# FP4 feed-forward stage in one fixed instruction order: output transposes inside a later tile's last quarter, input transposes between output products

## The chip, the cores and the metric

The kernel runs on one core of a Trainium2 chip. The metric is the device time in microseconds of one execution, the median of several runs. The kernel before has a median of 2238.77 us in three runs (2237.82 to 2240.83).

A core has five engines that run their own queues in order: TensorE (PE), VectorE (DVE), ScalarE (ACT), GpSimd (POOL) and SyncE (SP, which issues the DMAs here). They wait for each other through semaphores.

## What is computed

Two layers of gated cross attention and feed-forward over x (8 x 224 rows of 512). Only the last feed-forward is touched by the change:

```python
def fp4_quant_dequant(x):            # blocks of 16 along the last dim
    scale = max(|xb|) / 6, at least 1e-12
    q = nearest of {0, .5, 1, 1.5, 2, 3, 4, 6} to |xb / scale|, sign kept
    return q * scale
gate = fp4(x) @ fp4(w_gate).T        # 512 -> 1408
y    = fp4(x) @ fp4(w_up).T          # 512 -> 1408
h    = silu(gate) * y
out  = x + tanh(g) * (fp4(h) @ fp4(w_down).T)     # 1408 -> 512
```

In the kernel fp4 of x is taken after a layernorm. All products are in float32; each matrix product of the program is two records (two MATMUL and two LDWEIGHTS) in the profile, a transpose is one.

## The kernel before

**The stage.** The 1792 rows are 14 tiles of 128 rows (`NF`). A tile f goes through four functions:

- `ffn1_in` (L1035): a DMA loads x, three DVE passes and a POOL pass make the layernorm's statistics, a DVE pass normalizes, `fp4_steps` quantizes 512 columns, four PE transposes (L1055) go into a PSUM tile, and `evac` (L85) copies them into `xqT`, alternating between ACT and DVE.
- `ffn1_hidden` (L1059): the 1408 hidden columns are four quarters of 352. For each, four gate products (`wg`) go into one half of a PSUM tile and four up products (`wu`) into the other half, all at L1066. ACT makes a tanh of the gate half (L1077), DVE multiplies it with the gate half (L1078), and after the up products DVE multiplies with the up half (L1080) into h. In the last stage `banks` (L1172) hands out one PSUM tile `ps_big` for both halves, from a pool of two.
- `fp4_steps` (L939) on h, in two pieces of 704 columns: eight DVE passes (L959, L960, L961, L964, L967, L971, L972, L973) and one POOL pass (L974).
- `ffn1_out` (L1085): eleven PE transposes of h (L1092) in groups of 4, 4 and 3 through the PSUM tiles `th` and `t` (one buffer each), ACT copies into `hqT` (L1093), eleven output products of 512 columns with `wd` (L1097), a DVE add (L1109) and the store.

These functions are generators: each `yield` is a place where other work may be put in between.

**Order of the work.** `ffn1` (L1164) loops over tiles 2 to 13. One turn emits the hidden part of tile f, the input of tile f + 1, the quantization of h of tile f, and the output of tile f - 2, one after the other; the outputs of tiles 12 and 13 follow the loop. Tiles 0 and 1 have their input and hidden parts in `ffn1_first` (L1112) and `ffn1_head` (L1130), inside the last attention batch. There the two halves have separate PSUM tiles (L1154).

The emitted order is not the executed one everywhere. The framework schedules instructions and adds the semaphore waits. `pin` (L208) chains the PE, DVE and ACT instructions emitted so far in their order. It is called at L1305, before the last stage: what comes ahead of that keeps the order of the code, the last stage is ordered by the scheduler. In the order that results, the scheduler puts some gate products of the next quarter ahead of the up products of a quarter, and splits transposes and output products among them.

**Pace.** In the attention of the second layer `pace` (L251) takes pieces from the queue `beside` until the DVE work that is owed reaches a number of us, 3.5 at L652.

Of the kernel before, what the change touches and what calls it, by code (L numbers as in the profile page):

```python
# [26 lines left out]
F32 = mybir.dt.float32  # L27
# [7 lines left out]
B, S, D = 8, 224, 512  # L35
# [27 lines left out]
class Net:  # L63
# [492 lines left out]
    def attention8(self, n, soon, values, queue, beside):  # L556
# [50 lines left out]
        for slot in range(KC * NT):  # L607
            g, i = divmod(slot, NT)
            sc = [self.ps("half", [TP, 2, 512]) for _ in rows]
            for c in range(2):  # L610
                for h, r in enumerate(rows):
                    nc.tensor.matmul(  # L612
                        sc[h][:, c, :MH],
                        lhsT=qT[r, g, i * TP : (i + 1) * TP],
                        rhs=kT[g][r, c * MH : (c + 1) * MH],
                        start=True,
                        stop=True,
                    )
            nms = []
            for h in range(2):  # L620
                src = sc[h][:, :, :MH]
                mx = self.small.tile([TP, 1], F32, name="mx")
                nc.vector.tensor_tensor_reduce(  # L623
                    out=src,
                    in0=src,
                    in1=masks[i],
                    scale=1.0,
                    scalar=-MASKED,
                    op0=ALU.add,
                    op1=ALU.max,  # L630
                    accum_out=mx,
                )

                nms.append(self.small.tile([TP, 1], F32, name="nm"))
                nc.vector.tensor_scalar(nms[h], mx, -1.0e38, -1.0, ALU.max, ALU.mult)  # L635
            self.behind = 0
            if not soon:
                self.pace(1.5, beside)
            if slot == 4:
                next(first)  # L640
            p = self.weights_room(TP, M)
            for h, us in enumerate((1.6, 1.0)):
                self.fill(us, queue)
                nc.scalar.activation(  # L644
                    p[:, h, :].rearrange("p (c k) -> p c k", c=2),
                    sc[h][:, :, :MH],
                    AF.Exp,
                    bias=nms[h],
                    accum_out=total[:, i, h, g : g + 1],
                )  # L650
            if not soon:
                self.pace(3.5, beside)  # L652
            self.fill(1.6, queue)
            if slot == 3:
                first = divided(0)
                next(first)
            if slot == 4:
                next(first)
            if slot == 1:
                self.finish(values)  # L660
            if slot:
                product(*before)
            if slot == 4:
                next(first)
            pT = self.weights_room(CP, NKT * TP)
            for h in range(2):
                pt = self.ps("half", [CP, 2, 512])
                half = NKT // 2
                for j in range(NKT):
                    nc.tensor.transpose(  # L670
                        pt[:, j // half, j % half * TP : (j % half + 1) * TP],
                        p[:, h, j * CP : (j + 1) * CP],
                        self.ident[:TP, :TP],
                    )
                nc.scalar.copy(  # L675
                    pT[:, h, :].rearrange("p (c k) -> p c k", c=2), pt[:, :, : half * TP]
                )
            before = g, i, pT
            self.finish(soon)
            self.fill(1.2 if n < 2 * B - 1 else 3.0, queue)  # L680
# [354 lines left out]
    def ffn1_in(self, work, f, x, xn, xqT, bufs):  # L1035


        nc = self.nc
        nc.sync.dma_start(out=x, in_=self.last[f * TF : (f + 1) * TF, :])
        st = self.small.tile([TF, 6], F32, name="st1")  # L1040
        nc.vector.bn_stats(st, x)
        mv = self.small.tile([TF, 2], F32, name="mv1")
        nc.vector.bn_aggr(mv, st)
        ve = self.small.tile([TF, 1], F32, name="ve1")
        nc.vector.tensor_scalar(ve, mv[:, 1:2], EPS, None, ALU.add)
        rstd = self.small.tile([TF, 1], F32, name="rstd1")
        nc.gpsimd.tensor_tensor(rstd, ve, self.neghalf[:, 0:1], ALU.pow)
        yield 0, 1.2
        nc.vector.tensor_scalar(xn, x, mv[:, 0:1], rstd, ALU.subtract, ALU.mult)
        yield 0, 0.6  # L1050
        yield from self.fp4_steps(work, xn, xn, D, bufs)
        yield 0, 0, True
        pt = self.ps("t", [128, KC, TF])
        for k in range(KC):
            nc.tensor.transpose(pt[:, k, :], xn[:, k * 128 : (k + 1) * 128], self.ident)  # L1055
        self.evac(xqT, pt)
        yield 0.45, 0

    def ffn1_hidden(self, xqT, h, gate, banks):  # L1059
# [23 lines left out]
            yield 0.6, 0.6  # L1083

    def ffn1_out(self, pool, f, x, h, wd):  # L1085
        nc = self.nc
        hqT = pool.tile([128, NC1, TF], F32, name="hqT", bufs=2)

        def transposes(k0, k1, bank):
            pt = self.ps(bank, [128, k1 - k0, TF])  # L1090
            for k in range(k0, k1):
                nc.tensor.transpose(pt[:, k - k0, :], h[:, k * 128 : (k + 1) * 128], self.ident)  # L1092
            nc.scalar.copy(hqT[:, k0:k1, :], pt)  # L1093

        def products(k0, k1):
            for k in range(k0, k1):
                nc.tensor.matmul(  # L1097
                    po, lhsT=hqT[:, k, :], rhs=wd[:, k, :], start=k == 0, stop=k == NC1 - 1
                )


        transposes(0, 4, "th")
        transposes(4, 8, "t")
        po = self.ps("m", [TF, D])
        products(0, 4)
        transposes(8, NC1, "th")
        products(4, NC1)
        y = pool.tile([TF, D], F32, name="yout", bufs=2)
        nc.vector.scalar_tensor_tensor(y, po, self.gate[:, 3:4], x, ALU.mult, ALU.add)  # L1109
        nc.sync.dma_start(out=self.out[f * TF : (f + 1) * TF, :], in_=y)  # L1110
# [19 lines left out]
    def ffn1_head(self, work, beside):  # L1130
# [1 line left out]
        h = self.head  # L1132
        flat = self.wpool.tile([128, KC * D], F32, name="wv")
        h["h"].append(flat[:, :HID1])
        room = self.att.tile([128, KC, MH], F32, name="cx", bufs=2)
        room = room.rearrange("p k m -> p (k m)")
        at, there = 0, {}
        for name, width in (("a", D), ("e", D), ("most", D // BLK), ("scale", D // BLK), ("inv", D // BLK)):
# [3 lines left out]
        def quantized(h):  # L1142
            for c0 in range(0, HID1, D):
                part = h[:, c0 : min(c0 + D, HID1)]
                yield from self.fp4_steps(work, part, part, part.shape[1])

        for f in range(2):
            ahead = self.ffn1_in(there, f + 1, h["x"][f + 1], h["xn"], h["xqT"], 1)
            for i, cost in enumerate(
                self.ffn1_hidden(  # L1150
                    h["xqT"],
                    h["h"][f],
                    lambda: flat[:, HID1 : HID1 + CW],
                    lambda: [self.ps("m", [TF, CW]) for _ in range(2)],  # L1154
                )
            ):
                yield cost
                if i % 5 == 2 and i < 25:
                    yield next(ahead)
            yield from ahead  # L1160
            if f == 0:
                beside.append(quantized(h["h"][f]))

    def ffn1(self, pool, wd):  # L1164

        def quantized(h):
            for c0 in range(0, HID1, QW):
                self.fp4(pool, h[:, c0 : c0 + QW], h[:, c0 : c0 + QW], QW, 2)  # L1170

        def banks():  # L1172
            ps = self.ps("big", [TF, 2, 512])
            return ps[:, 0, :], ps[:, 1, :]

        x, h, xqT = self.head["x"], self.head["h"], self.head["xqT"]
        waiting = [(0, x[0], h[0]), (1, x[1], h[1])]
        x = x[2]
        quantized(h[1])
        for f in range(2, NF):  # L1180
            h = pool.tile([TF, HID1], F32, name="h", bufs=3)
            for _ in self.ffn1_hidden(
                xqT, h, lambda: pool.tile([TF, CW], F32, name="gth", bufs=2), banks
            ):
                pass
            waiting.append((f, x, h))
            if f + 1 < NF:
                x = pool.tile([TF, D], F32, name="xf", bufs=5)
                xn = pool.tile([TF, D], F32, name="xn1", bufs=2)
                xqT = pool.tile([128, KC, TF], F32, name="xqT1", bufs=2)  # L1190
                for _ in self.ffn1_in(pool, f + 1, x, xn, xqT, 2):
                    pass
            quantized(h)
            self.ffn1_out(pool, *waiting.pop(0), wd)
        for tile_ in waiting:
            self.ffn1_out(pool, *tile_, wd)

    def run(self):  # L1200
# [101 lines left out]
                self.weight("wo", sources[1]["wo"])  # L1302
        self.finish(beside)
        self.finish([rest, self.project_out(2 * B - 1)])
        self.pin()  # L1305
        prep.close()
        banks.close()
        right.close()
# [1 line left out]
        with ExitStack() as last:  # L1310
# [2 lines left out]
            wd = wdpool.tile([128, NC1, D], F32, name="wd")  # L1313
            self.nc.sync.dma_start(out=wd, in_=self.wd)
            self.ffn1(self.pool(last, "ffn1", side="right"), wd)


# [67 lines left out]
```

## Time and profile before

| what | value |
|---|---|
| median of three runs | 2238.77 us |
| the profiled execution's own time | 2234.42 us |
| its span, first to last instruction | 2232.6 us |
| mean granted PE clock | 0.998 |
| PE busy, share of the span | 2151.8 us, 96% |
| DVE busy | 1385.0 us, 62% |
| ACT busy | 699.2 us, 31% |
| POOL busy | 130.7 us, 6% |
| chain that ended last: PE | 84% |
| chain that ended last: DVE | 12% |
| last stage, loop over tiles 2 to 13 | 1828.35 to 2206.44 us |

How to read it: the span is cut by the profiler into instructions with a start and a duration for each engine. "Idle before" an instruction is followed by the instruction that released it. Matmuls overlap: a record of PE has its own length, about 0.17 us longer than the distance to the next one in a dense row, so rates are read from starts. PE's weight loads have a row of their own (PEld) and run beside products.

### The profile page before, as it was taken

Reading aid. Unit: us, or ns where it says so; the run is one execution under the profiler, and the core shown is the slowest. Engines: PE = TensorE matmul, PEld = TensorE weight load, DVE = VectorE, ACT = ScalarE, POOL = GpSimd, SP = SyncE. Lnnn points to the kernel's source line nnn. Section 1 sums busy time; section 2 is a strip of 40 time slices with the busy share of each in tenths; the row PEclk is TensorE's granted clock in tenths of the full one; section 3 lists DMA queues with packets and bytes.
Section 4 is the critical chain, followed back from the end, with each engine's and each line's share of the span. In section 5 each row is a group of like instructions: output and inputs, shape, how many; then the busy total and the mean of one; then the engine's idle time right before and its main releaser. Section 6 shows DMA issues by size and latency. Waiting matters only on the chain.

```text
span 2232.6 us, 33189 instructions
## 1 busy us (share of the span) xinstructions
PE 2151.8 (96%) x14062; PEld 1226.2 (55%) x14062; DVE 1385.0 (62%) x2618; ACT 699.2 (31%) x1173; POOL 130.7 (6%) x145
## 2 busy tenths in 40 slices
PE   7989899999999999999899999999999999999999
PEld 4444546364555546465656565665656555555554
DVE  3786767676766767773656565564523468666652
ACT  1222415151423325152543343343434321110111
POOL 0000000000000000000001010110000012111110
PEclk9999999999999999999999999999999999999999
DMA  6210010101000011101011212122110020000000
GB/s 218 67 38 29 1 45 2 31 15 30 16 18 29 7 39 39 63 2 63 3 38 57 63 28 64 41 67 66 37 36 15 9 85 10 5 20 19 19 5 19
DMA packets 48628, 81.30 MB, mean 36 GB/s; under 512 B 3296, under 2 KB 27616, under 8 KB 48352
## 3 DMA queue, kind: packets, MB, share of 16 engines
q1 hardware_dynamic: 48480, 79.18, 11.3%
q8 instruction: 110, 1.80, 0.3%
q14 instruction: 38, 0.31, 0.0%
HBM read 65.28 MB, written 13.89 MB: 35 GB/s over the span
## 4 chain that ended last, share of the span: by engine, by line
PE 84%; DVE 12%; ACT 2%; issue 1%; DMA 1%; SPq 0%; POOL 0%; ACTq 0%; DVEq 0%
PE ps_m L354 14%; PE ps_m L293 12%; PE ps_big L1066 7%; PE ps_pa L515 6%; PE ps_m L1097 6%; PE ps_m L378 5%; PE ps_quad L461 4%; PE ps_half L612 4%; PE ps_m L322 4%; PE ps_half L670 4%; PE ps_pa L575 4%; PE ps_quad L438 3%; PE ps_t L813 2%; DVE part L468 2%; PE ps_m L1066 2%; PE ps_quad L429 1%
## 5 line engine op out<-in xcount | busy, mean ns | idle before, releaser
L293 PE MATMUL ps_m<-cx,wk 128*128 128x375 f32 x1024 | 362.4, 487 | 10.0 <-DMA wk<-in_L_Wk 10.0
L354 PE MATMUL ps_m<-wv,cx 128*125 128x512 f32 x768 | 354.5, 602 | 0.0
L623 DVE CUSTOM_DVE_ANT_0 ps_half<-ps_half,mbias 112x750 f32<-112x750 f32 x128 | 121.1, 946 | 292.1 <-PE ps_half L612 291.8
L468 DVE TENSOR_REDUCE part<-ps_quad 112x4 f32<-112x1500 f32 x128 | 220.0, 1719 | 127.0 <-PE ps_quad L461 127.0
L293 PEld LDWEIGHTS ps_m<-cx,wk 128*128 128x128 f32 x1024 | 182.4, 191 | 110.8 <-issue 28.3
L354 PEld LDWEIGHTS ps_m<-wv,cx 128*125 128x125 f32 x768 | 136.1, 187 | 173.8 <-issue 168.8
L504 ACT ACTIVATE p<-ps_quad 125x1792 f32<-125x1792 f32 x96 | 159.7, 1664 | 198.8 <-PE ps_quad L438 198.8
L363 ACT COPY v<-ps_m 125x512 f32<-125x512 f32 x96 | 56.1, 585 | 439.0 <-PE ps_m L354 433.8
L1097 PE MATMUL ps_m<-wd,hqT 128*128 128x512 f32 x308 | 138.3, 595 | 3.8 <-ACT hqT L1093 3.1
L644 ACT ACTIVATE p<-ps_half,nm 112x750 f32<-112x750 f32 x128 | 113.1, 888 | 47.6 <-DVE nm L635 41.7
L675 ACT COPY p<-ps_half 125x672 f32<-125x672 f32 x128 | 85.8, 722 | 131.6 <-PE ps_half L670 131.6
L461 PE MATMUL ps_quad<-kT,qT 32*112 32x375 f32 x1024 | 115.3, 519 | 11.8 <-DVE part L468 11.8
L378 PE MATMUL ps_m<-wo,aT 128*112 128x512 f32 x256 | 120.4, 601 | 0.0
L1066 PE MATMUL ps_big<-wg,xqT 128*128 128x352 f32 x352 | 115.4, 463 | 1.8 <-DVE h L1080 1.4
L1066 PE MATMUL ps_big<-wu,xqT 128*128 128x352 f32 x352 | 113.7, 466 | 0.8 <-DVE gth L1078 0.8
L837 DVE SCALAR_TENSOR_TENSOR y<-hp,cw,y 128x224 f32<-128x224 f32 x256 | 109.5, 449 | 4.5
L322 PE MATMUL ps_m<-xnT,wq 128*128 128x224 f32 x512 | 107.9, 357 | 0.6 <-ACT xnT L186 0.6
L515 PE MATMUL ps_pa<-p,v 125*32 125x224 f32 x1536 | 93.3, 361 | 14.8 <-ACT p L504 14.8
L1077 ACT ACTIVATE gth<-ps_big 128x352 f32<-128x352 f32 x48 | 22.2, 463 | 257.2 <-PE ps_big L1066 234.1
L670 PE MATMUL ps_half<-ident,p 112*125 112x112 f32 x768 | 99.9, 280 | 0.0
L612 PE MATMUL ps_half<-kT,qT 64*112 64x375 f32 x512 | 98.5, 498 | 0.9 <-ACT p L675 0.9
L322 PEld LDWEIGHTS ps_m<-xnT,wq 128*128 128x128 f32 x512 | 93.7, 190 | 9.4 <-issue 5.3
(199 smaller groups left out, 2873.7 us busy)
## 6 DMA issues: line engine op xcount, KB each, us to landing
cx<-in_ctx SPq DMA_DIRECT2D x32, 750.0 KB, 4.3
wst<-in_w SPq DMA_DIRECT2D x16, 512.0 KB, 7.8
x<-in_x SPq DMA_DIRECT2D x8, 448.0 KB, 7.0
mid<-x SPq DMA_DIRECT2D x8, 448.0 KB, 3.1
x<-mid SPq DMA_DIRECT2D x8, 448.0 KB, 3.5
last<-x SPq DMA_DIRECT2D x8, 448.0 KB, 3.1
out<-yout SPq DMA_DIRECT2D x14, 256.0 KB, 2.0
wraw<-in_w_gate SPq DMA_DIRECT2D x11, 256.0 KB, 2.6
```

The costliest lines, as they stand in the source:

```text
L293: nc.tensor.matmul(pk, lhsT=self.w["wk"][:, k, g * 128 : (g + 1) * 128], rhs=job["cx"][c][:, k, :], start=k == 0, stop=k == KC - 1,)
L322: nc.tensor.matmul(pq[:, g - g0, :], lhsT=self.w["wq"][:, k, g * 128 : (g + 1) * 128], rhs=xnT[:, k, :], start=k == 0, stop=k == KC - 1,)
L354: nc.tensor.matmul(pv, lhsT=job["cx"][c][:, k, at : at + CP], rhs=self.w["wv"][:, k, :], start=k == 0, stop=k == KC - 1,)
L378: nc.tensor.matmul(po, lhsT=aT[:, g, i * TP : (i + 1) * TP], rhs=self.w["wo"][:, g, :], start=g == 0, stop=g == KC - 1,)
L461: nc.tensor.matmul(sc[:, h, :MH], lhsT=qT[r, g, i * TP : (i + 1) * TP], rhs=kT[g][r, c * MH : (c + 1) * MH], start=True, stop=True,)
L468: nc.vector.tensor_reduce(part[:, i, g, :, c], sc[:, :, :MH], AX.X, ALU.max)
L504: nc.scalar.activation(p, pw[:, :, : 2 * S], AF.Exp)
L515: nc.tensor.matmul(pa[r, which, :], lhsT=self.ones[:CP, r] if which else job["v"][j][:, col : col + 32], rhs=p[:, h, (j - j0) * S : (j - j ...
L612: nc.tensor.matmul(sc[h][:, c, :MH], lhsT=qT[r, g, i * TP : (i + 1) * TP], rhs=kT[g][r, c * MH : (c + 1) * MH], start=True, stop=True,)
L670: nc.tensor.transpose(pt[:, j // half, j % half * TP : (j % half + 1) * TP], p[:, h, j * CP : (j + 1) * CP], self.ident[:TP, :TP],)
L1066: nc.tensor.matmul(ps[:, :CW], lhsT=xqT[:, k, :], rhs=wt[:, k, c0 : c0 + CW], start=k == 0, stop=k == KC - 1,)
L1097: nc.tensor.matmul(po, lhsT=hqT[:, k, :], rhs=wd[:, k, :], start=k == 0, stop=k == NC1 - 1)
```

## The change

The last stage is written in the order in which it is to run, and `pin` is called after it instead of before it, so that this order is kept on PE, DVE and ACT.

- The output of tile f - 2 becomes a generator with four parts: transposes 0 to 7, transposes 8 to 10, five products, six products. In turn f the first part is placed ahead of the gate products of the last quarter (step 23), the second behind these gate products (step 27) and ahead of the up products; the first five products follow the last up product, then come the transposes of the input of tile f + 1, then the other six.
- The input of tile f + 1 up to its quantization is placed in turn f at steps 1, 4, 6, 9, 12 and 14 of the hidden part.
- The quantization of h of tile f - 1 (no longer f) is placed at steps 10, 15, 17, 20, 22 and 25. A quarter has eight steps, 0 to 7 in the first; the fourth stands behind L1078, the eighth behind L1080.
- The last two outputs are interleaved with each other.
- The copies into `xqT` always run on ACT.
- In the head stage the two inputs ahead use a second `xqT` buffer, and their steps are placed at every fourth step instead of every fifth.
- In the last attention batch the pace after slot 1 is 2.5 instead of 3.5.

```diff
-                self.pace(3.5, beside)
+                self.pace(3.5 if n + 1 < 2 * B or slot < 2 else 2.5, beside)
...
-        self.evac(xqT, pt)
+        nc.scalar.copy(xqT, pt)
...
         transposes(0, 4, "th")
         transposes(4, 8, "t")
+        yield
+        transposes(8, NC1, "th")
+        yield
         po = self.ps("m", [TF, D])
-        products(0, 4)
-        transposes(8, NC1, "th")
-        products(4, NC1)
+        products(0, 5)
+        yield
+        products(5, NC1)
...
-        room = self.att.tile([128, KC, MH], F32, name="cx", bufs=2)
+        room, other = (self.att.tile([128, KC, MH], F32, name="cx", bufs=2) for _ in range(2))
...
+        other = other.rearrange("p k m -> p (k m)")[:, :D].rearrange("p (k t) -> p k t", k=KC)
+        xqTs = [h["xqT"], other, h["xqT"]]
         for f in range(2):
-            ahead = self.ffn1_in(there, f + 1, h["x"][f + 1], h["xn"], h["xqT"], 1)
+            ahead = self.ffn1_in(there, f + 1, h["x"][f + 1], h["xn"], xqTs[f + 1], 1)
...
-                    h["xqT"],
+                    xqTs[f],
...
-                if i % 5 == 2 and i < 25:
+                if i % 4 == 2 and i < 27:
                     yield next(ahead)
...
-                self.fp4(pool, h[:, c0 : c0 + QW], h[:, c0 : c0 + QW], QW, 2)
+                yield from self.fp4_steps(pool, h[:, c0 : c0 + QW], h[:, c0 : c0 + QW], QW, 2)
...
-        waiting = [(0, x[0], h[0]), (1, x[1], h[1])]
-        x = x[2]
-        quantized(h[1])
+        waiting = [self.ffn1_out(pool, f, x[f], h[f], wd) for f in range(2)]
+        x, last = x[2], h[1]
         for f in range(2, NF):
+            out = waiting.pop(0)
             h = pool.tile([TF, HID1], F32, name="h", bufs=3)
-            for _ in self.ffn1_hidden(
-                xqT, h, lambda: pool.tile([TF, CW], F32, name="gth", bufs=2), banks
+            if f + 1 < NF:
+                xf = pool.tile([TF, D], F32, name="xf", bufs=5)
+                xn = pool.tile([TF, D], F32, name="xn1", bufs=2)
+                xT = pool.tile([128, KC, TF], F32, name="xqT1", bufs=2)
+                ahead = self.ffn1_in(pool, f + 1, xf, xn, xT, 2)
+            steps = quantized(last)
+            for i, _ in enumerate(
+                self.ffn1_hidden(
+                    xqT, h, lambda: pool.tile([TF, CW], F32, name="gth", bufs=2), banks
+                )
             ):
+                if f + 1 < NF and i in (1, 4, 6, 9, 12, 14):
+                    next(ahead)
+                if i in (10, 15, 17, 20, 22, 25):
+                    next(steps)
+                if i in (23, 27):
+                    next(out)
+            for _ in steps:
                 pass
-            waiting.append((f, x, h))
+            waiting.append(self.ffn1_out(pool, f, x, h, wd))
+            next(out)
             if f + 1 < NF:
-                x = pool.tile([TF, D], F32, name="xf", bufs=5)
-                xn = pool.tile([TF, D], F32, name="xn1", bufs=2)
-                xqT = pool.tile([128, KC, TF], F32, name="xqT1", bufs=2)
-                for _ in self.ffn1_in(pool, f + 1, x, xn, xqT, 2):
+                for _ in ahead:
                     pass
-            quantized(h)
-            self.ffn1_out(pool, *waiting.pop(0), wd)
-        for tile_ in waiting:
-            self.ffn1_out(pool, *tile_, wd)
+                x, xqT = xf, xT
+            else:
+                for _ in quantized(h):
+                    pass
+                next(waiting[0])
+            for _ in out:
+                pass
+            last = h
+
+        first, second = waiting
+        next(first)
+        next(first)
+        next(second)
+        for _ in first:
+            pass
+        next(second)
+        for _ in second:
+            pass
...
-        self.pin()
         prep.close()
...
             self.ffn1(self.pool(last, "ffn1", side="right"), wd)
+            self.pin()
```

## The prediction

> **What bounds the kernel now.** The change works in the last stage: twelve loop turns, tiles 2 to 13 of the FP4 block. I took the stretches first: from the first gate product of that loop (1828.35 us) to the end of its last turn (2206.44), and from there to the end of the span. Columns: us, then busy time and count of PE, weight load, DVE, ACT and POOL, the granted clock, DMA.
>
> ```profile
> 1828.35:2206.44 378.09, 370.25 (x1211) 211.43 (x1210) 249.02 (x454) 44.17 (x89) 54.76 (x48) 1.00 0.06 19
> 2206.44:2232.60 26.16, 21.82 (x66) 10.33 (x64) 2.25 (x3) 3.10 (x6) 0.00 (x0) 1.00 0.08 30
> ```
>
> PE is busy 370 of 378 us, at full clock; DVE 249. So PE bounds the loop, and one turn takes 378.09 / 12 = 31.51 us. What would PE need with no gap? From starts that follow each other in PE's timeline: eight products of 352 columns (16 records, 1828.35 to 1833.08) are 0.591 us each, seven of 512 columns (2043.87 to 2049.88) 0.859, a transpose 0.11 (four in 0.44). A turn has 32, 11 and 15 of them: 18.91 + 9.45 + 1.65 = **30.01 us**. Only 1.5 us of a turn can be won, 18 us in all.
>
> Why that little is lost now shows in the timeline of all engines at the start of one turn (start, duration, engine, line, operation, tiles, shapes, records; two records are one product):
>
> ```profile
> 2049.88 3.71 PE L1066 MATMUL ps_big<-wg,xqT 128*128 128x352 f32 x12
> ...
> 2052.45 0.46 ACT L1077 ACTIVATE gth<-ps_big 128x352 f32<-128x352 f32 x1 [7.90 <-PE ps_big L1066]
> 2052.95 0.52 DVE L1078 SCALAR_TENSOR_TENSOR gth<-gth,ps_big 128x352 f32<-128x352 f32 x1 [2.11 <-ACT gth L1077]
> 2053.52 2.07 PEld L1066 LDWEIGHTS ps_big<-wu,xqT 128*128 128x128 f32 x8 [0.49 <-DVE gth L1078]
> 2053.52 2.63 PE L1066 MATMUL ps_big<-wu,xqT 128*128 128x352 f32 x8
> ```
>
> The four gate products of this quarter are streamed by 2049.88 + 8 x 0.2955 = 2052.24. The up products start only at 2053.52, 0.05 us after DVE's L1078 has ended. They wait for it: both halves of `ps_big` are one tile, and in the built program the first up product of a quarter has a wait on L1078 of the same quarter. The list of waits from 1930 us to the end says it too:
>
> ```profile
> PEld ps_big L1066 <- DVE gth L1078: 8.6, 21, 0.5
> PEld ps_big L1066 <- DVE h L1080: 6.1, 12, 0.8
> ```
>
> (total, times, longest). The wait is short since the scheduler has put two gate products of the next quarter ahead of the up products: 12 records before `wu`, not 8. The chain ACT, DVE lies beside those.
>
> **The change, part by part.** Durations come from the profiled execution (span 2232.6 us, its own time 2234.42; the three runs have a median of 2238.77, 4.35 more, which I add at the end).
>
> *The pin moved to the very end.* Now PE, DVE and ACT run the last stage in the order written. In the changed kernel's built order PE has, in all twelve turns, 4 gate, 4 up, 4 gate, 4 up, and each first up product still waits for its own L1078. Behind that product all of PE is queued, and only PE's work is late. So four times a turn PE stands from the end of the gate products to the end of L1078: 2053.52 - 2052.24 = **1.28 us**, if ACT and DVE are free. After such a wait eight records take 2.47 us until the next start (2053.52 to 2055.99), not 2.36: 0.1 more.
>
> What is DVE doing then? In the new order it is as follows (S: start of the up products of the quarter before; they end at S + 2.46, L1080 runs S + 2.68 to 3.20, the next gate products end at S + 4.82; DVE passes without a dependence overlap by 0.08):
> - quarter 0: only the output add (0.75) and three statistics passes; free in time: 1.28.
> - quarter 1: after L1080 come two 512-wide passes (1.1 us) and three small ones on 704 (1.5): L1078 starts at S + 5.7, the up products at S + 6.25: 1.43.
> - quarter 2: after L1080 come five 704-wide passes. Their rows in the present timeline:
>
> ```profile
> 2064.47 0.89 DVE L964 SCALAR_TENSOR_TENSOR q_a<-h,q_inv 128x704 f32<-128x704 f32 x1
> 2065.39 0.53 DVE L967 TENSOR_SCALAR q_e<-q_a 128x704 int32<-128x704 int32 x1
> 2065.95 0.53 DVE L971 TENSOR_SCALAR q_e<-q_e 128x704 f32<-128x704 f32 x1
> 2066.52 0.89 DVE L972 TENSOR_TENSOR q_a<-q_a,q_e 128x704 f32<-128x704 f32 x1
> ...
> 2067.76 0.88 DVE L973 TENSOR_TENSOR q_a<-q_a,q_e 128x704 f32<-128x704 f32 x1
> ```
>
>  With the 0.04 between dependent passes they are 3.85 us: 3.12 + 3.85 - 0.08 puts L1078 at S + 6.9, the up products at S + 7.45: **2.6 us**. This is the dearest spot: a block of quantization stands ahead of the pass PE waits for.
> - quarter 3: the three transposes of the previous output (0.33) lie inside the wait: 1.28 - 0.33 = 0.95; DVE is done at about the same time.
>
> Sum 1.28 + 1.43 + 2.6 + 0.95 + 4 x 0.1 = 6.66 us; a turn is 30.01 + 6.66 = 36.67. Twelve turns: 440.0 - 378.1 = **+61.9 us**. Bounds: with DVE never late the stalls are 3 x 1.28 + 0.95 + 0.4 = 5.2, a turn 35.2, so +44.4. All of it is on the path that ends last, since PE has no other work in its queue.
>
> *Transposes moved, copies on ACT.* Same count on PE, and the waits of before for hqT and xqT copies (3.1 and 1.2 us from 1860 us on) are gone; that is in the 30.01. ACT has 0.59 us more every other turn, but is busy 44 of 378 us; cover: six output products (5.2 us) between the input transposes and the next gate products; without it 0.7 us a turn.
>
> *DMAs.* The loads of x stand a turn and more ahead of use in the SP order, behind output stores only: nothing. The first load of the loop waits for the old pools; its 2.9 us delay DVE in turn 2 by under 1 us.
>
> *The end.* Two tiles of 11 products and 11 transposes, 2 x 10.66 = 21.3 us, now 22.4 (2206.28 to 2228.69): **-1.1**; the quantization of tile 13 lies beside 14.9 us of products.
>
> *Ahead of the loop (pace 2.5, the second xqT buffer, earlier input steps).* The wait of 2.18 us for the xqT copy at 1783.45 goes. But DVE has two more quantization pieces (some 4 us) ahead of the pass L601 that the last projection waits for; of these PE can cover about 1.7 us by the two products that need the first half only: +2. Net 0, from -4 (both waits of 2.2 us there go) to +3.
>
> *The clock.* PE has not had such gaps in this loop before. Elsewhere it has:
>
> ```profile
> 1799.84 3.69 PE L1066 MATMUL ps_m<-wg,wq 128*128 128x352 f32 x6 [2.20 <-DVE wv L1078]
> ```
>
> ```profile
> 1801.00:1802.00 1.00, 1.00 (x3) 0.58 (x2) 0.96 (x3) 0.00 (x0) 0.00 (x0) 0.50 0.00 0
> ```
>
> (first the timeline, then the microsecond from 1801 among the stretches.) After 2.20 us of idle PE the granted clock is 0.50 for some 3.3 us, and three products take 3.62 us where 1.77 is normal: 1.75 lost with the restart taken off. Of nine gaps of 1.8 to 2.4 us in this trace two were followed by it (1799.84, and 144.22 with 0.58). With a gap of 2.6 us a turn I take two in nine: 12 x 2/9 x 1.75 = **+4.7**; bounds 0 and 21 (every turn).
>
> The Trainium skill, "TensorE: Matmul & The Clock Gate", section "Why this matters for your kernels", allows gaps up to about 3 us before the clock is halved. By it the clock term would be 0; the row above shows a halving after 2.20 us, so the row decides and the rule does not lower the sum. The skill's "PSUM — Partial Sum Buffer", section "PSUM bank collisions raise a hardware error", asks to guard by bank and partition group; the two halves of `ps_big` are two banks, so by that rule no up product need wait and the loop would come near 30 us a turn. The wait in the built program and the row at 2053.52 say it does wait.
>
> Sum: 61.9 - 1.1 + 0 + 4.7 = +65.5; 2234.42 + 65.5 = 2299.9 for a profiled execution, 4.35 more as a median: **2304 us**.
>
> **Rivals.**
> - *DVE is never late* (blocks of quantization fit into PE's waits better than I have it): +44.4 - 1.1 = 2277.7, as a median 2282. For it: DVE is busy only 249 of 378 us. Against: its order is now fixed, and five passes stand ahead of L1078.
> - *The clock is halved every turn*: 61.9 - 1.1 + 21 = 2316.2, as a median 2321. For it: 2.6 us is longer than any gap in the trace that did not halve it (2.39). Against: seven of nine gaps passed.
> - *Not slower: the up products don't have to wait.* The place is the first up product of each quarter; the price is the stall there. If it is under 1.5 us a turn, 0.37 a quarter, the fixed order wins. At nothing: 12 x 30.01 = 360.1, -18 - 1.1: 2215.3, as a median 2220. For it: in the stage before, with two separate tiles, `wu` follows `wg` directly (1783.45, 1785.92). Against: the built wait, and no up product from 2044 to 2108 that starts before its L1078 has ended.
> - *The order doesn't reach the chip or costs nothing net*: within 0.2% (4.5 us, about what a measurement here can tell from no change). The built order speaks against it.
>
> **How the numbers follow.** Forecast (2292 to 2313) 0.50; DVE never late 0.20; clock every turn 0.20; up products free, faster, 0.07; within 0.2% 0.03. Slower in all: 0.90. The range runs from the DVE floor with the best case ahead of the loop (2282 - 4, and 2 for scatter) to the clock bound with the worst (2321 + 3 + 2): 2276 to 2326.
>
> **What would show it.** In the profile after: idle PE ahead of L1066 put down to DVE gth L1078 of some 75 us over the loop, four per turn, 1.3, 1.4, 2.6 and 0.9 long; turns of 36 to 37 us; DVE q_a L973 just ahead of the late L1078; clock below 1.00 in a few stretches. Wrong if turns are near 30 us with `wu` starting before L1078 ends, or if the gap of quarter 2 is no longer than the others.

## The result and the profile after

| | median | lowest to highest | profiled execution: own time, span, clock |
|---|---|---|---|
| before | 2238.62 us (5 runs) | 2236.4 to 2240.83 | 2234.42, 2232.6, 0.998 |
| after | 2320.45 us (5 runs) | 2314.0 to 2322.94 | 2321.88, 2320.1, 0.99 |

The change makes the kernel slower: ratio 1.0366, 95% interval 1.0354 to 1.0379. The forecast was 2304, its range 2276 to 2326.

First the same stretches as before: the loop, then its end, then the first turn alone, and two microseconds that are used further down.

```profile
1838.65:2294.85 456.20, 384.50 (x1215) 217.65 (x1214) 244.98 (x445) 47.08 (x97) 52.19 (x47) 0.97 0.05 16
2294.85:2320.10 25.25, 21.46 (x61) 9.94 (x59) 4.75 (x7) 2.04 (x4) 1.38 (x1) 0.99 0.08 31
1838.65:1882.91 44.26, 33.15 (x102) 18.70 (x101) 20.20 (x37) 3.88 (x8) 4.37 (x4) 0.92 0.17 57
1976.00:1978.00 2.00, 2.00 (x5) 1.04 (x4) 1.80 (x3) 0.00 (x0) 0.00 (x0) 0.50 0.00 0
```

The loop takes 456.20 us, not 378.09. PE did 370 us of work in it before and has the same work now; what is new is 72 us in which it is idle and some that it spends at a lower clock. The list of waits, from 1838 us to the end, has one line (total, times, longest):

```profile
PE ps_big L1066 <- DVE gth L1078: 71.7, 48, 6.7
```

48 waits are four in each of twelve turns, one for each quarter. One turn that nothing disturbs, from 1995.93 to 2032.53, in the timeline of all engines:

```profile
1995.93 2.53 PE L1066 MATMUL ps_big<-wg,xqT 128*128 128x352 f32 x8
...
1998.50 0.46 ACT L1077 ACTIVATE gth<-ps_big 128x352 f32<-128x352 f32 x1 [6.88 <-PE ps_big L1066]
1998.99 0.52 DVE L1078 SCALAR_TENSOR_TENSOR gth<-gth,ps_big 128x352 f32<-128x352 f32 x1 [1.10 <-ACT gth L1077]
...
1999.57 2.63 PE L1066 MATMUL ps_big<-wu,xqT 128*128 128x352 f32 x8 [1.11 <-DVE gth L1078]
...
2005.74 2.63 PE L1066 MATMUL ps_big<-wu,xqT 128*128 128x352 f32 x8 [1.17 <-DVE gth L1078]
...
2008.21 2.53 PE L1066 MATMUL ps_big<-wg,xqT 128*128 128x352 f32 x8
...
2010.78 0.46 ACT L1077 ACTIVATE gth<-ps_big 128x352 f32<-128x352 f32 x1 [5.70 <-PE ps_big L1066]
2010.89 0.89 DVE L972 TENSOR_TENSOR q_a<-q_a,q_e 128x704 f32<-128x704 f32 x1
2011.82 0.89 DVE L973 TENSOR_TENSOR q_a<-q_a,q_e 128x704 f32<-128x704 f32 x1
2012.63 0.51 DVE L1078 SCALAR_TENSOR_TENSOR gth<-gth,ps_big 128x352 f32<-128x352 f32 x1
...
2013.20 2.63 PE L1066 MATMUL ps_big<-wu,xqT 128*128 128x352 f32 x8 [2.46 <-DVE gth L1078]
...
2020.18 2.63 PE L1066 MATMUL ps_big<-wu,xqT 128*128 128x352 f32 x8 [0.78 <-DVE gth L1078]
```

Each `wu` row begins 0.05 to 0.06 us after an L1078 has ended. In the first quarter that pass waits for ACT, which waits for the gate products: the plain chain. In the third, ACT is done at 2011.24, but DVE is in L972 and L973 until 2012.71: five quantization passes stand ahead of L1078 in DVE's queue.

### The profile page after: what moved, and what is told of

Its sections match the earlier page's. It is cut to its first block, busy times and chain, and to the rows that moved or that the text cites. A ratio compares the mean times of both kernels' runs of the same rounds, so it can differ in the third digit from the quotient of the medians.

```text
span 2320.1 us, 33192 instructions
## 1 busy us (share of the span) xinstructions
PE 2170.8 (94%) x14062; PEld 1233.6 (53%) x14062; DVE 1384.1 (60%) x2611; ACT 701.9 (30%) x1180; POOL 129.5 (6%) x145
## 4 chain that ended last, share of the span: by engine, by line
PE 83%; DVE 13%; ACT 2%; issue 1%; DMA 1%; SPq 0%; POOL 0%; ACTq 0%; DVEq 0%
PE ps_m L354 13%; PE ps_m L293 12%; PE ps_big L1066 8%; PE ps_pa L515 6%; PE ps_m L1098 6%; PE ps_m L378 5%; PE ps_quad L461 4%; PE ps_half L612 4%; PE ps_m L322 4%; PE ps_half L670 4%; PE ps_pa L575 3%; PE ps_quad L438 3%; PE ps_t L813 2%; DVE part L468 2%; PE ps_m L1066 1%; PE ps_quad L429 1%
## 5 line engine op out<-in xcount | busy, mean ns | idle before, releaser
L1066 PE MATMUL ps_big<-wu,xqT 128*128 128x352 f32 x352 | 125.7, 504 | 60.6 <-DVE gth L1078 60.6
L1066 PEld LDWEIGHTS ps_big<-wu,xqT 128*128 128x128 f32 x352 | 68.3, 204 | 114.3 <-DVE gth L1078 81.7
L322 PE MATMUL ps_m<-xnT,wq 128*128 128x224 f32 x512 | 107.9, 357 | 0.6 <-ACT xnT L186 0.6
L1077 ACT ACTIVATE gth<-ps_big 128x352 f32<-128x352 f32 x48 | 22.2, 463 | 253.3 <-PE ps_big L1066 239.8
```

Source lines behind the costliest of these rows:

```text
L322: nc.tensor.matmul(pq[:, g - g0, :], lhsT=self.w["wq"][:, k, g * 128 : (g + 1) * 128], rhs=xnT[:, k, :], start=k == 0, stop=k == KC - 1,)
L1066: nc.tensor.matmul(ps[:, :CW], lhsT=xqT[:, k, :], rhs=wt[:, k, c0 : c0 + CW], start=k == 0, stop=k == KC - 1,)
```

## The experiments

The first product of the last attention batch's queries (L322) lies in code that is the same in all kernels here, yet it starts between 1691.8 and 1699.1 us of the span from one profiled execution to the next. So "the head" below is the time from that product to the first gate product of the loop: 1828.35 - 1692.14 = 136.21 us before, 1838.65 - 1699.06 = 139.59 after. Most of this scatter is half clock ahead of that product, which falls differently in each execution (last section). Medians of different kernels are compared with it in mind. A, B and C in the expectations are rival theories, each with what it would make of the run. A turn of the loop is taken from its first gate product to that of the next turn.

| kernel | median, us | ratio to before, interval | head, us | loop |
|---|---|---|---|---|
| before | 2238 | | 136.21 | turn 31.51 |
| after | 2320.45 | 1.0366 (1.0354 to 1.0379) | 139.59 | turn 36.60, first 44.26 |
| e1 two tiles | 2223.36 | 0.9945 (0.9926 to 0.9964) | 139.60 | turn 30.02 |
| e2 steps late | 2293.60 | 1.0259 (1.0239 to 1.0279) | 141.37 | turn 35.25 |
| e3 pin at its old place | 2235.03 | 0.9988 (0.9976 to 1.0000) | 139.59 | 31.07 |
| e4 before, pinned | 2418.62 | 1.0823 (1.0805 to 1.0842) | 136.14 | turn 46.7 |
| e5 first input later | 2314.37 | 1.0343 (1.0324 to 1.0362) | 139.66 | first 38.94 |
| e6 two tiles, old head | 2216.01 | 0.9903 (0.9889 to 0.9916) | 133.05 | 30.02 |
| e7 two tiles, old pace | 2217.60 | 0.9909 (0.9896 to 0.9923) | 138.65 | 30.02 |
| e8 two tiles, rest first | 2219.08 | 0.9916 (0.9903 to 0.9930) | 136.44 | 30.02 |
| e9 before, two tiles | 2230.64 | 0.9964 (0.9951 to 0.9977) | 134.56 | turn 30.56, first two 33.6 |
| e10 e6, pin at its old place | 2217.83 | 0.9899 (0.9884 to 0.9914) | 134.69 | 30.1 |
| e11 e6, second xqT buffer | 2214.03 | 0.9888 (0.9875 to 0.9902) | 133.05 | 30.02 |

### e1: the wait taken away

```diff
-            ps = self.ps("big", [TF, 2, 512])
-            return ps[:, 0, :], ps[:, 1, :]
+            return self.ps("big", [TF, 512]), self.ps("big", [TF, 512])
...
-            self.psum_pool(last, big=2, th=1)
+            self.psum_pool(last, big=4, th=1)
```

> The changed kernel with one thing different: in the last stage the gate half and the up half of a quarter are two PSUM tiles of their own (four in the pool, the same space), no longer two halves of one tile. The order of PE, DVE and ACT stays that of the changed kernel. Theory A (the loss is the wait of the first up product for the DVE pass L1078 of the same quarter, which is there only because both halves are one tile): the four gaps of 1.1, 1.2, 2.5 and 0.8 us a turn go, a turn falls from 36.6 to 30.1 to 30.5 us, no half-clock stretch is left after the third gap, and the median is 2225 to 2245 us. Rival B (the fixed order costs the time by itself, since DVE's or ACT's queue is late in it whatever the up products wait for): the idle PE time moves to other lines, turns stay at 35 us or more, the median at 2300 or more. Rival C (half way: gate products now wait for the tile that was used two quarters ago): turns of 32 to 34 us, 2250 to 2280.

2223.36 us, 97.1 less than the changed kernel, below the kernel before and a little below the range of theory A. The stretch of the loop, then a quarter in the timeline:

```profile
1837.89:2198.10 360.21, 360.21 (x1216) 214.29 (x1215) 248.93 (x445) 47.14 (x97) 52.92 (x47) 1.00 0.06 20
```

```profile
1987.99 2.53 PE L1066 MATMUL ps_big<-wg,xqT 128*128 128x352 f32 x8
...
1990.36 2.53 PE L1066 MATMUL ps_big<-wu,xqT 128*128 128x352 f32 x8
...
1991.06 0.52 DVE L1078 SCALAR_TENSOR_TENSOR gth<-gth,ps_big 128x352 f32<-128x352 f32 x1 [1.11 <-ACT gth L1077]
```

PE is busy in all 360.21 us. `wu` now starts 0.70 us ahead of L1078. It writes another half than the one that L1077 and L1078 read, so no data asks for the old wait: it came with the shared tile, for it is gone with nothing else changed. 360.21 / 12 = 30.02 a turn, the 30.01 that the prediction worked out as PE's need. Theory A holds; B and C fall. The orders of PE, DVE and ACT are those of the changed kernel, so a fixed order costs nothing by itself.

### e2: the third gap

```diff
-                if i in (10, 15, 17, 20, 22, 25):
+                if i in (10, 15, 19, 20, 22, 27):
```

> The changed kernel with the quantization of h placed at steps 10, 15, 19, 20, 22 and 27 instead of 10, 15, 17, 20, 22 and 25: the pieces are the same, but the piece with the five passes of 704 columns no longer stands whole ahead of L1078 in the third quarter. Theory A (the third gap is 2.46 us long since DVE's quantization passes stand ahead of L1078 in its queue, and the half clock follows that gap alone): the third gap falls to 1.1 to 1.3 us, no eight up products take over 4 us in the loop after its first turn, a turn is 35.2 to 35.4 us, and the median falls by 20 to 30 us to some 2290 to 2300. Rival B (the third gap has another cause, such as the transposes or the copies on ACT): the gap stays near 2.5 and the median at 2315 to 2325. Rival C (the half clock comes from the number of gaps, not their length): the gap shrinks, the half-clock stretches stay, and the median falls by 12 to 16 us only.

2293.60 us, 26.9 less. The third quarter of one turn:

```profile
2002.11 0.46 ACT L1077 ACTIVATE gth<-ps_big 128x352 f32<-128x352 f32 x1 [5.70 <-PE ps_big L1066]
2002.61 0.52 DVE L1078 SCALAR_TENSOR_TENSOR gth<-gth,ps_big 128x352 f32<-128x352 f32 x1 [0.95 <-ACT gth L1077]
2003.05 0.52 DVE L971 TENSOR_SCALAR q_e<-q_e 128x704 f32<-128x704 f32 x1
...
2003.18 2.63 PE L1066 MATMUL ps_big<-wu,xqT 128*128 128x352 f32 x8 [1.11 <-DVE gth L1078]
```

L971 and what follows it now stand behind L1078; the gap is 1.11 and not 2.46 us, a turn is 35.25, and no eight up products behind the first turn take over 2.63 us. 12 x 1.35 = 16.2 us less waiting, and the rest of the gain is the half clock that had followed those gaps (9.8 us, below). Theory A holds; C, which ties the half clock to the number of gaps, falls.

### e3 and e4: the pin by itself, with new and with old order

```diff
+        self.pin()
         with ExitStack() as last:
...
-            self.pin()
```

> The changed kernel with the pin put back ahead of the last stage, where it was before: the written order of the change stays, but the scheduler is free to move instructions in the last stage. Theory A (the loss comes from the fixed order, that keeps the gate products of the next quarter behind the up products): the scheduler puts gate products of the next quarter ahead of the up products again, the gaps go, turns are 31 to 32 us, and the median is 2235 to 2250. Rival B (the new places of transposes, copies and quantization cost it): turns stay above 35 us, and the median above 2300.

2235.03 us, the kernel before to within what can be told. With the scheduler free again, one wait for L1078 is left:

```profile
PE ps_big L1066 <- DVE h L1080: 2.1, 5, 0.9
PE ps_big L1066 <- DVE gth L1078: 1.1, 1, 1.1
```

```profile
2177.74 3.71 PE L1066 MATMUL ps_big<-wg,xqT 128*128 128x352 f32 x12
2181.38 2.63 PE L1066 MATMUL ps_big<-wu,xqT 128*128 128x352 f32 x8
```

The 12 records ahead of `wu` are the old picture: two gate products of the next quarter fill the time of ACT and DVE. So the new places of transposes, copies and steps don't cost the 80 us; the pin does, together with the shared tile.

The kernel before with its pin moved to the end:

```diff
-        self.pin()
         with ExitStack() as last:
...
+            self.pin()
```

> The kernel before with one thing different: the pin is called at the very end, so that the order in which the old code writes the last stage is kept. Theory A (a fixed order costs what its waits cost, and the moved transposes and steps of the change take some of them out): four waits of the up products for L1078 a turn, about 1.1 to 1.3 us each, and besides PE waits for the whole input chain of the next tile and for the copies into hqT, some 8 to 10 us a turn: turns of 42 to 46 us, a median of 2370 to 2440. Rival B (the moves of the change are worth nothing in a fixed order): about the time of the changed kernel, 2310 to 2330.

2418.62 us, a turn 46.7 on average from the second on (longer than theory A's 42 to 46; its other half, the waits, is right). Two waits make most of it:

```profile
PE ps_t L1055 <- POOL xn L974: 92.9, 11, 8.5
PE ps_big L1066 <- DVE gth L1078: 62.5, 48, 10.4
```

The old order written out has the 48 waits for L1078 as well, and the input transposes wait some 8.4 us a turn for the whole chain of layernorm and quantization. Half clock follows each of these long waits and adds to them. The change's moves are worth 98 us of what the pin costs the old order (2418.62 - 2320.45); rival B falls.

### e5: the first turn

```diff
-                if f + 1 < NF and i in (1, 4, 6, 9, 12, 14):
+                if f + 1 < NF and i in ((1, 4, 6, 9, 12, 14) if f > 2 else (11, 12, 13, 20, 28)):
```

> The changed kernel with one thing different: in the first turn of the loop alone, the input steps of tile 3 stand at 11, 12, 13, 20 and 28 instead of 1, 4, 6, 9, 12 and 14. So the DVE pass L1041 that waits for the load of x no longer stands ahead of the first quarter's L1078. Theory A (the first turn is 7.7 us longer than the others since the up products wait for L1078, L1078 stands behind L1041 in DVE's queue, and L1041 waits for a load issued only when the attention's last x is stored): the first gap of the first turn falls from 6.7 to about 1.2 us, its eight up products take 2.63 us and not 4.70, the third gap may grow to 3 us, the first turn is 36.6 to 38.5 us instead of 44.3, and the median falls by 5.5 to 8 us to 2312 to 2315. Rival B (something else at the start of the loop holds PE, such as the load of wd, which runs at the same time): the first turn stays at 42 us or more, the median within 2 us of the changed kernel.

In the changed kernel the first quarter of the loop, in the timeline:

```profile
1838.65 2.53 PE L1066 MATMUL ps_big<-wg,wq 128*128 128x352 f32 x8
...
1839.63 0.32 SPq L153 DMA_DIRECT2D last<-x  x1
1840.06 3.35 SPq L1039 DMA_DIRECT2D xf<-last  x5
1841.27 0.46 ACT L1077 ACTIVATE gth<-ps_big 128x352 f32<-128x352 f32 x1 [13.53 <-DMA wd<-wd_quantized]
1846.31 0.69 DVE L1041 BATCH_NORM_STATS2 st<-xf 128x6 f32<-128x512 f32 x1 [6.71 <-DMA xf<-last]
...
1847.33 0.51 DVE L1078 SCALAR_TENSOR_TENSOR gth<-gth,ps_big 128x352 f32<-128x352 f32 x1
...
1847.89 4.70 PE L1066 MATMUL ps_big<-wu,wq 128*128 128x352 f32 x8 [6.71 <-DVE gth L1078]
```

The loads of x are issued from 1840.06, behind the store of the attention's last x. L1041 takes the first of them at 1846.31; L1078, which could have run from 1841.73 when ACT was done, stands behind it, and PE behind that. (ACT's own wait is put down to the load of `wd`, but L1077 starts just as the gate products end.) In the kernel before, DVE had other work at this place:

```profile
1828.54 0.32 SPq L1039 DMA_DIRECT2D xf<-last  x1
1829.22 1.67 DVE L959 TENSOR_REDUCE q_most<-wv 128x44 f32<-128x704 f32 x2
...
1839.00 1.28 DVE L1041 BATCH_NORM_STATS2 st<-xf 128x6 f32<-128x512 f32 x2
```

With the input steps later (e5):

```profile
1831.60 2.53 PE L1066 MATMUL ps_big<-wg,wq 128*128 128x352 f32 x8
1835.29 2.63 PE L1066 MATMUL ps_big<-wu,wq 128*128 128x352 f32 x8 [1.16 <-DVE gth L1078]
```

The first turn is 38.94 and not 44.26 us, a little over what theory A put (its third gap is 3.12, with half clock behind it), and the median is 6.1 lower. Theory A holds; the load of `wd`, which runs at the same time in both, is not the cause.

### e6, e7, e8, e11: the edits ahead of the last stage

All four start from e1, where the loop is at PE's need, so that what is left is the head.

```diff
-                self.pace(3.5 if n + 1 < 2 * B or slot < 2 else 2.5, beside)
+                self.pace(3.5, beside)
...
-        xqTs = [h["xqT"], other, h["xqT"]]
+        xqTs = [h["xqT"]] * 3
...
-                if i % 4 == 2 and i < 27:
+                if i % 5 == 2 and i < 25:
```

> The kernel with two PSUM tiles, and in it the three edits ahead of the last stage undone: pace 3.5 throughout, one buffer for xqT, the head stage's input steps at every fourth... as before, every fifth step. Theory A (these three edits together cost time: they take the wait of 2.18 us for the xqT copy away, but give waits of 0.95, 3.12, 1.91 and 2.97 us behind DVE in its place): the waits of PE in the last 70 us ahead of the loop fall from 9.0 to some 5.5 us, the loop starts some 3.4 us earlier against the end of the common code, turns stay at 30.0, and the median is 2218 to 2221, against 2223.4 with the two tiles alone. Rival B (the edits are worth nothing or a gain; the later start of the loop was a difference between executions): the median is 2223 or more.

2216.01 us, 7.4 less than e1; the head is 139.60 - 133.05 = 6.55 shorter. The waits of PE in the last part of the head, first of the changed kernel, then of e6:

```profile
PE ps_m L1066 <- DVE wv L1078: 4.1, 2, 3.1
PE ps_m L378 <- DVE aT L601: 3.0, 1, 3.0
PE ps_t L417 <- DVE stat L407: 1.9, 1, 1.9
```

```profile
PE ps_m L1066 <- DVE wv L1078: 2.4, 2, 2.2
PE ps_t L417 <- ACT wq L1056: 0.9, 1, 0.9
PE ps_m L1066 <- ACT wq L1056: 0.7, 1, 0.7
```

4.1 + 3.0 + 1.9 = 9.0 against 4.0, and the first kernel runs its output projection's twelve records behind the wait of 2.97 us in 6.95 us, where 16 take 7.03 in e6: half clock, 1.6 us more. So theory A holds, and the edits cost more than it had put (5 us of waits, 1.6 of clock). The kernel before had 2.18 and not 0.7 us for the xqT copy: that copy was on DVE, behind other passes. Putting it on ACT, the one edit of the head that e6 keeps, is the useful one: the head is 3.16 shorter than in the kernel before (1.5 us less waiting for that copy; the rest is half clock, 1.75 us there and none in this execution).

e7 undoes the pace alone (the first hunk above).

> The kernel with two PSUM tiles, and in it one of the three edits ahead of the last stage undone: the pace of the last attention batch is 3.5 throughout. Theory A (the smaller pace leaves quantization pieces of h to the end of the head, where five to eight of their passes stand ahead of L601, for which the last projection waits): the wait of 2.97 us for L601 falls under 1 us, while the others stay or grow a little, and the median is 1 to 3 us below the 2223.4 of the two tiles alone. Rival B (the waits come from the earlier input steps, not from the pace): the wait for L601 stays near 3 us, or what it gives up turns up at an L1078, and the median stays at 2222 to 2226.

2217.60 us, 5.8 less: more than either theory put it. The wait for L601 is gone, as A says; the longest wait for L1078 is 3.34 and not 3.12. The trace explains only 1 us of the 5.8 (head 138.65), since that execution has two half-clock stretches that cost about 3 us. Over all runs, span times mean granted clock has a median of 2213.6 in e1 and 2211.4 here: by this estimate some 2 us are the work of the edit, as theory A put it, and the rest is where half clock happened to fall.

e8 leaves the pace and moves the rest of the quantization behind the attention's end.

```diff
-        self.finish(beside)
         self.finish([rest, self.project_out(2 * B - 1)])
+        self.finish(beside)
```

> The kernel with two PSUM tiles, and in it one thing different: what is left of the quantization of h of tile 0 is emitted behind the end of the last attention batch and its projection, not ahead. So eleven DVE passes (some 6 us) stand behind L601 and the adds L389, no longer ahead of L601; PE's order is the same. Theory A (the wait of 2.97 us for L601 comes from these passes): it falls to 0.5 us or less, the passes lie beside the first quarters of the loop, where up products no longer wait for L1078 of their own quarter, and the median falls by 2 to 3.5 us to 2220 to 2221.5. Rival B (moved, they make the first quarters late, since a gate product needs the tile that the L1080 of two quarters back frees, or hold back the load of wd that needs their room): a wait of 2 us or more in the first turn, the median unchanged or higher.

2219.08 us, 4.3 less, the head 3.2 shorter; no wait for L601, and none in the loop (half clock behind an earlier wait takes 1.6 us of the gain in this execution). Theory A (2 to 3.5 us less) holds: those DVE passes ahead of L601 are where the smaller pace is paid for.

e11 is e6 with the second buffer made again (only the middle hunk of e6 taken back).

> The same fastest kernel with one of the edits ahead of the last stage made again: the second buffer for xqT. Pace and input steps stay the old ones. Theory A (the buffer only lets the four input transposes run before the last up products, and so takes away the wait of 0.68 us ahead of the first gate product; the cost of the three edits lies in the earlier steps and the smaller pace): that wait goes, no wait for DVE is longer than in the fastest kernel, the loop starts 0.4 to 1 us earlier against the common code, and the median is 2214 to 2216. Rival B (the buffer itself costs, since a wait of DVE's or PE's moves with the transposes): the median is 2217 or more.

2214.03 us, its interval over e6's; the head is 133.05 in both, and the wait of 0.68 us is still there. The buffer does nothing by itself: theory A's reason falls, B too. The loss (6.55 us in the head) lies in the earlier steps and the pace.

### e9 and e10: is the fixed order worth anything?

e9 is the kernel before with the edit of e1.

> The kernel before with one thing different: in its last stage the gate half and the up half of a quarter are two PSUM tiles (four in the pool, the same space). The scheduler still orders the last stage. Theory A (what the kernel before lost in its loop, 1.5 us a turn, was the same wait of the up products for L1078, hidden in part by the scheduler's order; so the two tiles give most of the gain without any fixed order): turns of 30.0 to 30.7 us, a median of 2220 to 2228 against 2238 before. Rival B (the scheduler's order has waits of its own, for copies, transposes and L1080, that only the written order removes): turns of 31 us or more, a median of 2231 to 2239; the fixed order is then worth the rest of the way to 2216.

2230.64 us: between the two theories. From the third turn a turn is 30.56 us, as A says; but the first two take 67.2 us together (3.3 us of waits, and half clock from 1859.25 to 1866.07), and each later turn keeps waits that B named. From 1892 to 2210 us:

```profile
PE ps_t L1092 <- DVE xqT L91: 2.7, 5, 1.3
PE ps_t L1092 <- ACT xqT L89: 1.2, 4, 0.3
PE ps_m L1097 <- ACT hqT L1093: 0.6, 2, 0.3
```

These are what the moved transposes and the ACT copies were made to remove, and in e6 they are gone.

e10 is e6 with the pin at its old place.

> The fastest kernel so far (two PSUM tiles, written order kept, the edits ahead of the last stage undone; 2216.0 us) with the pin put back ahead of the last stage, so that the scheduler may reorder the last stage. Theory A (with two tiles the written order has no wait left on PE, so that nothing the scheduler does can be better than 30.0 us a turn): the same or slower, 2215 to 2224. Rival B (the scheduler's order starts the loop earlier, by work moved into the last waits of the head): faster, 2211 to 2214.

2217.83 us, the interval over e6's. With two tiles the written order and the scheduler's are worth the same, and the gain of e6 over e9 (14.6 us) is that of the order in which the code is written and of the ACT copies, not of the pin.

## Why the prediction was right, and where its sizes were off

The profiled span grew by 87.5 us: 6.9 ahead of the first query product, in code that is the same; 3.4 in the head; 78.1 in the loop; -0.9 at the end. The prediction's sum was +65.5 over a profiled time. By the number alone one could take the result for another case: 2320.45 lies outside the 2292 to 2313 that the forecast gave half its chance, and all but on the rival "the clock is halved every turn" (2321). The trace says no to that rival: half clock followed six of the twelve third gaps, and cost 9.8 us, not 21. What came true is the forecast's own wait; the rest of the way was made by terms that it had too small. By its steps:

- **The wait** (right). It read from the built program and from one row that the up products wait for their own L1078, and that the new order has nothing to put in between. 48 waits on that line; e1 takes away what makes them and 97 us go. Its rival "the up products don't have to wait", at 2220 us, is close to the time of that kernel (2223.36): a right price for another program.
- **The four stalls** (right). Put at 1.28, 1.43, 2.6 and 0.95 us; measured from the end of the gate products (8 x 0.2955 after their start) they are 1.28, 1.34, 2.63 and 0.95. The idle times in the profile, 1.11, 1.17, 2.46 and 0.78, are 0.17 less, since a record of PE ends later than its products stream. A turn is 36.60 (put at 36.67): 12 x (36.60 - 31.51) = 61.1, put at 61.9. The reason for 2.6, L973 just ahead of L1078, is in the rows and in e2.
- **The clock** (mechanism right, size too small). Two in nine gaps were put to be followed by half clock, 4.7 us. Of the twelve gaps of 2.46 us six were (not the first turn's), and those turns take 38.13 to 38.30: 9.8 us. Nine gaps of 1.8 to 2.4 us were too few, and too short, to size this; what decides is in the last section.
- **The first turn** (this step failed). "Its 2.9 us delay DVE in turn 2 by under 1 us" priced the first load at DVE and did not follow it on to PE: L1041 stands ahead of L1078 in DVE's queue, and PE behind L1078. The turn is 7.7 longer than the others: 6.71 - 1.11 = 5.6 of waiting, 4.70 - 2.63 = 2.1 of half clock. In the kernel before, DVE had sixteen quantization passes to do at that place (1829.22 to 1838.2), and the load was beside them; the change moved these passes later and so took its cover away.
- **Ahead of the loop** (put at 0, up to +3; measured +3.4). The wait for the xqT copy did go, by 2.2, as said, and L601 was late, as said, by 2.97 and not 2. Missed were the three pieces of DVE's work that the earlier steps put ahead of the L1078 of the stage itself and of L407: 0.95, 3.12 and 1.91 us of waiting where it was 0.22, 2.20 and 0.88. Half clock costs about the same in both: behind the 2.20 us gap before, behind the wait for L601 after.
- **The end** (right): -1.1 put, -0.9 measured.

The parts of the loop: 61.1 + 9.8 + 7.7 - 0.5 (the last turn has no input transposes) = 78.1. What the total was short of lies in the three terms above (5 + 7 + 3 us) and in the 6.9 us ahead of the first query product, most of which is half clock as well (last section). As medians, 2304 against 2320.45, the forecast is 16.4 short.

## What to carry to other kernels

Before an order is fixed, ask for each wait on the engine that bounds: what stands behind it in the queue, and does the data ask for it, or does a tile that two things share? Here splitting one tile in two (at the same space) turned 3.7% slower into 0.5% faster, with PE's, DVE's and ACT's instructions in the same order. And where DVE feeds PE in a fixed order, a load that is waited for on DVE is waited for by PE: put what may be late behind the pass that PE needs.

## What the runs showed of the hardware

Half clock after short gaps. A turn whose gap of 2.46 us was followed by it, in the changed kernel:

```profile
1974.90 4.33 PE L1066 MATMUL ps_big<-wu,xqT 128*128 128x352 f32 x8 [2.46 <-DVE gth L1078]
```

Eight records take 4.33 where 2.63 is normal, and from 1976 to 1978 the granted clock is 0.50 (the fourth of the stretches at the top). The length of a gap does not decide alone. Gaps of 1.2 us and less were never followed by it (over 100 in the loops of the changed kernel, e2 and e5); one of 1.90 was (e7, at 1820.89); of 2.45 to 2.46, six of twelve in the changed kernel and seven of eleven in e5; of about 8.4, all eleven in e4. The same gap of some 3.12 us in the head was followed by it in e2, e5 and e8 and not in e1, e3 and the changed kernel.

What decides can be read from the clock as the traces record it. In each of the thirteen profiled executions the half-clock stretches that end inside the span last 3.41 us or two or three times that, and all begin on one grid with a step of 3.413 us. Some windows of this grid in the changed kernel (columns as at the top; the first number behind the length is busy PE, the third from the end the clock):

```profile
1971.55:1974.96 3.41, 0.95 (x5) 0.28 (x3) 3.31 (x6) 0.46 (x1) 0.46 (x1) 1.00 0.00 0
1974.97:1978.37 3.40, 3.40 (x6) 2.10 (x7) 2.77 (x5) 0.00 (x0) 0.91 (x1) 0.50 0.00 0
1978.38:1981.79 3.41, 3.41 (x18) 2.42 (x17) 2.46 (x4) 1.08 (x2) 0.00 (x0) 1.00 0.00 0
2009.10:2012.51 3.41, 1.64 (x6) 0.76 (x4) 3.27 (x5) 0.46 (x1) 0.00 (x0) 1.00 0.00 0
2012.51:2015.92 3.41, 2.72 (x11) 1.83 (x12) 3.27 (x7) 0.00 (x0) 1.39 (x1) 1.00 0.00 0
```

The gap before 1974.90 lies in one window, 3.41 - 0.95 = 2.46 us of idle PE, and the next window has half clock. The gap of the same length before 2013.20 is cut by a window's end into 1.77 and 0.69 us, and the clock stays. Over all thirteen executions, every full-clock window with 1.99 us or more of idle PE was followed by half clock (55 of 55), none with less than 1.80 us was (of 8311), and 10 of the 44 between were. Half clock ended behind windows with 0.35 us of idle or less and went on behind those with 0.55 or more. (Idle is what PE's records leave free, and their ends are modelled, so the bounds are good to some 0.2 us.) From these numbers, as an estimate: a gap of 2.46 us puts 1.9 us or more into one window in (3.41 + 2.46 - 2 x 1.9) / 3.41 = 0.61 of its possible places; 13 of 23 were seen.

The same explains the scatter between executions. Before the first query product of the last batch the kernel before has one window of half clock and the changed kernel four; three more, at half of 3.41 us each, are 5.1 of the 6.9 us. Over the thirteen executions that product starts at 1691.8 to 1692.3 behind one such window, at 1694.3 behind two, at 1696.3 to 1697.4 behind three and at 1698.3 to 1699.1 behind four.

The Trainium skill, "TensorE: Matmul & The Clock Gate", section "What's actually happening", has a window of 3413 ns that runs free of the kernel. The traces agree: the grid has this step, and its place in the span differs from one execution to the next. Its bound of one whole idle window is not what these runs show: 1.99 us of idle in a window was enough each time, and gaps of 1.90 and 2.46 us are shorter than the window.
